# First products of the second layer on GpSimd, their sums two turns later; softplus in pairs

## Chip, cores and metric

The kernel runs on one core of a Trainium2 chip, as one program. The metric is the device time of one execution in microseconds; the median of three runs is given, and a profiled execution beside it.

## What is computed

Two layers, each behind a group norm and with a residual sum, on x of 4 x 256 x 64 x 128 (batch, time, rows, channels) in float32. The first is a pair of selective scans (forward and backward in time) with a gated output, a layer norm and a small MLP; the second makes a kernel per position out of a convolution and mixes with it.

```python
# layer 0, per row: L = 256 steps, 256 inner channels, 16 states
u = silu(causal_conv(xc, cw, cb))
xdbl = u @ Wx.T
dt = softplus(xdbl[..., :8] @ Wdt.T + bdt)
# per step: h = exp(dt * A) * h + (dt * u) * B ; y = sum over n of h * C
y = selective_scan(u, dt, -exp(Al), Bm, Cm, Dv) * silu(z)
...
# layer 1, per position: NH = 8 heads, DK = DV = DD = 16
xp = silu(x @ W1) @ W2                       # q (8 x 16), k (16), v (16), each normed
K_H1 = conv2d(k, H1_w).reshape(-1, DK, DD) + P1
kernel = einsum('xnk,xkd->xnd', q, K_H1)
feature = conv2d(v, H2_w); V_G = conv2d(v, G_w) + I
feature = einsum('xvw,xvd->xwd', V_G, feature)
out = einsum('xnd,xvd->xvn', kernel, feature)
```

## The kernel before

**Layer 0.** The rows are taken two at a time: a group G is 512 columns (two rows of 256 steps), 32 groups make one batch entry, 128 groups the whole. Each group has 32 units (G, i, n), one per direction i and state n, 4096 in all. The main loop (line 993) is one turn per unit k: turn k traces, for the unit three ahead, the broadcast of its C row from DRAM (`rows_of_c`, line 464, on SP's queue) and its operands (`inputs`: four dbt on ScalarE at line 472, a memset of one column on GpSimd at line 476, two exponentials "decay" on ScalarE at line 478); TensorE's transposes of dbt into one of three banks db (`turned`, line 492); the two scans on VectorE (`scanned`, line 504), which read decay from SBUF and db from PSUM; the weighting of the scanned states by C on GpSimd (`weighted`, line 510); and, for the unit two turns back, the transposing sums into the banks y (`added`, line 532). dbt, decay, hs and cc have four buffers each.

**The streams.** All the rest is written as generators that take steps between the units. A `yield 1, n` ends a turn's step, and n is how many of the three free PSUM banks ("mm", lists `free`, `take`, `give`) the next step needs; without them the stream waits. `front` makes a group's operands: transposes and norms, the convolution into u, silu, and per direction dt with its softplus, du = dt times u on GpSimd (line 418) and its transposes. A front starts 50 turns ahead of its group (LEAD); if it is not ready in time, the loop steps all the streams again in the same turn (line 1035). `back` takes the finished y through gate, projection, norms and MLP: xo is written at lines 571 and 574, x1 = MLP + xo at line 615, its statistics and its transposes follow, and x1 goes to DRAM. `project` starts the second layer on chunks of 512 positions: q, k and v, with the squares on GpSimd (line 690) and their sums on VectorE (line 693). A batch entry's chunks can begin when its whole first layer is done. `mix` takes the projected chunks four blocks of 128 positions at a time.

**A block of `mix`.** Filters: TensorE convolves k and v into one bank `fil` (`filters`, line 750). First product: `products` (line 755) multiplies q, repeated over d, with the filter's first 256 columns, repeated over heads, 2048 elements, into the single buffer pr. First sum: line 840 reduces these to ker, 128 columns. Second product (line 755 again) of the filter's other half with ker, and the bank is given back. Second sum at line 851, the outer product at line 766 and the gathering by TensorE at line 777; the result is copied to o at line 862. Between these stand `yield`s, so a block is spread over several turns. While the mixing is behind its plan (line 1023), it has two steps in every fourth turn. Blocks that are left when the loop ends go through `mix_alone`, which has an order of its own and has its first products on GpSimd already (line 925).

**Order.** Instructions go to the engines' queues by a list scheduler, which follows the program's order where operands are ready in its own estimate of time and takes later ones first where they are not. Two things bind it by hand: `tc.keep_in_program_order(ins)` puts an instruction behind the one traced before it on its engine, and `with tc.issue_after(ins)` puts what the block traces on that engine behind `ins`; neither waits for completion. The engines run their queues in order.

**Activation tables.** Exp and Ln share a table; silu, gelu and softplus need others. `both_tables` (line 204) loads the shared one by hand; where a function's table is not there, a load stands on the function's own line. `softplus` (line 305) is called once per group, with the dt of both directions, then takes any waiting gelu.

Of the kernel before, what the change touches and what calls it, by code (L numbers as in the profile page):

```python
# [13 lines left out]
F32 = mybir.dt.float32  # L14
AF = mybir.ActivationFunctionType
ALU = mybir.AluOpType
AX = mybir.AxisListType
# [9 lines left out]
NH, DK, DV, DD = 8, 16, 16, 16  # L27
# [5 lines left out]
COLS = 512  # L33
# [6 lines left out]
def fused_kernel(ctx: ExitStack, tc: tile.TileContext, a: dict, out: bass.AP):  # L40
    nc = tc.nc
# [90 lines left out]
    with tc.tile_pool(name="prep", bufs=1) as prep:  # L132
        w_in = prep.tile([128, DI], F32, name="w_in")
        nc.sync.dma_start(out=w_in, in_=a["W_inT"][:, 0:DI])
        for i, s in enumerate(("", "b")):
# [9 lines left out]
            na = const.tile([128, 2, NS], F32, name=f"neg_a{i}")  # L145
# [16 lines left out]
    p1 = ctx.enter_context(tc.tile_pool(name="p1", bufs=1))  # L162
# [26 lines left out]

    free = list(banks)  # L190
    norms = []

    def take():
        return free.pop(0)
# [4 lines left out]
    def later(turns):  # L199
        for _ in range(turns):  # L200
            yield 1, 0
# [101 lines left out]
            nc.vector.tensor_scalar(to, bank, bias, None, ALU.add)  # L303

    def softplus(*ts):
        for dt in ts:
            nc.scalar.activation(dt, dt, AF.Softplus)  # L307
        gelu()
        both_tables()

# [184 lines left out]
    def scanned(k):  # L495
        G, i, n = units[k]
        st = state[G]
        hs = st["hs", i, n] = p4.tile([128, 2, COLS], F32, name="hs")
        da = st.pop(("da", i, n)).rearrange("d (h s) t -> d h (s t)", h=2)
        for h in range(2):  # L500
            d0, d1, dh = da[:, h, :], dbs[(2 * k + h) % 3], hs[:, h, :]
            if i == 1:
                d0, d1, dh = d0[:, ::-1], d1[:, ::-1], dh[:, ::-1]
            nc.vector.tensor_tensor_scan(dh, d0, d1, 0.0, ALU.mult, ALU.add)  # L504

    def weighted(k):
        G, i, n = units[k]
# [34 lines left out]
    def back(G):  # L542

        b, g = divmod(G, NGRP)
# [25 lines left out]
        xo = p1.tile([128, COLS], F32, name="xo")  # L570
# [40 lines left out]
            )  # L611
        turned_x(m2, xin, add=True)
        yield 1, 0
        x1 = p1.tile([128, COLS], F32, name="x1")
        nc.vector.scalar_tensor_tensor(x1, m2, b2m, xo, ALU.add, ALU.add)
        give(m2)
        yield 1, 1
# [131 lines left out]
                    dst = dst.rearrange("p (k d) -> p d k", k=cn)  # L749
            nc.tensor.matmul(dst, lhsT=lhsT, rhs=wt, start=start and t == 0, stop=t == 2, skip_group_check=True)  # L750

    def products(left, right, na, nb):

        pr = p1.tile([128, na, nb, 16], F32, name="pr")
        nc.vector.tensor_tensor(  # L755
            pr,
            left.rearrange("p (a e) -> p a e", e=16)[:, :, None, :].to_broadcast([128, na, nb, 16]),
            right.rearrange("p (b e) -> p b e", e=16)[:, None, :, :].to_broadcast([128, na, nb, 16]),
            ALU.mult,
        )  # L760
        return pr

    def outer(eng, pr, left, right, na, nb):
# [42 lines left out]
    def mix():  # L806

        blocks = [(K, j) for K in range(B * NCHK) for j in range(CB)]
        fil = None

        def filters(K, j):
            f = take()
            convolved(f[:, 0:256], 0, K, j, True, True)
            convolved(f[:, 256:512], 1, K, j, False)
            return f

        for at, (K, j) in enumerate(blocks):
            if j == 0 and len(cols) > 1:
                return
            w = chunk.get(K)  # L820
            if j == 0 and "operands" not in (w or {}):
                while not ready(K):
                    yield 1, 0
                    if len(cols) > 1:
                        return
                w = chunk[K]
                operands(K)
                yield from later(3)
            if j == 0:
                o = p1.tile([128, CB, C], F32, name="o")  # L830
                x1 = loaded_x1(K)
            qkv = w["qkv"]
            if fil is None:
                yield 1, 1
                fil = filters(K, j)
                yield 1, 0
            pr = products(qkv[:, j, 0 : NH * DK], fil[:, 0:256], NH, DD)
            yield 1, 0
            ker = p1.tile([128, NH * DD], F32, name="ker")
            nc.vector.tensor_reduce(ker.rearrange("p (n d) -> p n d", d=DD), pr, AX.X, ALU.add)  # L840
            yield 1, 0
            pr = products(fil[:, 256:512], ker, DV, NH)
            give(fil)
            fil = None
            yield 1, 1
            gat = take()
            convolved(gat[:, 0:256], 2, K, j, True)
            if j == CB - 1 and len(cols) == 1 and ready(K + 1):
                operands(K + 1)
            nv = p1.tile([128, DV * NH], F32, name="nv")  # L850
            nc.vector.tensor_reduce(nv.rearrange("p (v n) -> p v n", n=NH), pr, AX.X, ALU.add)  # L851
            yield 1, 0
            pr = p1.tile([128, DV, C], F32, name="pr")
            outer(nc.vector, pr, by(gat[:, 0:256]), by(nv, NH), DV, NH)
            give(gat)
            yield 1, 1
            ot = take()
            gathered(ot[:, 0:128], pr, x1[:, j : j + 1, :])
            if j + 1 < CB and free:
                fil = filters(*blocks[at + 1])  # L860
            yield 1, 0
            nc.scalar.copy(o[:, j, :], ot[:, 0:128])
            give(ot)
            if j == CB - 1:
                w["mixed"] = True
                yield 1, 1
                yield from finish(K, o)
# [125 lines left out]
    for k in range(len(units) + LAG):  # L993
        G, at = divmod(k, UNITS)
        b, g = divmod(G, NGRP)
# [118 lines left out]
```

## Time and profile before

| | us |
|---|---|
| median of three runs (19493.19 to 19508.58) | 19500.96 |
| the profiled execution | 19461.56 |
| its span | 19459.8 |
| first scan starts / last scan starts | 198.8 / 18083.6 |
| first sum at line 840, first / last start (376 of them) | 4430.4 / 18189.8 |
| sums of `mix_alone` (line 908), first / last start (136) | 18242.2 / 19447.9 |

| engine, line | what | count | busy us | mean ns |
|---|---|---|---|---|
| GpSimd 510 | weighting | 4096 | 9717.3 | 2375 |
| VectorE 504 | scan | 8192 | 9503.4 | 1203 |
| ScalarE 472 | dbt | 16384 | 7051.8 | 499 |
| ScalarE 478 | decay | 8192 | 5443.3 | 711 |
| TensorE 492 | transposes into db | 32768 | 4999.5 | 284 |
| TensorE 532 | transposing sums into y | 32768 | 4453.2 | 280 |
| GpSimd 418 | du | 256 | 617.6 | 2412 |
| GpSimd 766 | outer products of `mix_alone` | 272 | 544.6 | 2028 |
| ScalarE 204 | table loads by hand | 420 | 538.9 | 1283 |
| ScalarE 307 | table loads at softplus | 195 | 250.2 | 1283 |

How to read it: "busy" is the time in which an engine works on instructions of the program; "idle before" is the engine's idle time just ahead of an instruction, and what is named behind an arrow is the event that ended it ("issue": nothing that the profile shows). Means over the whole run mix stages with different limits, so the same views are also taken over windows, counted in us from the span's start. Some records are missing from a trace: 374 of the 376 first products carry their operands' names.

### The profile page before, as it was taken

What the parts mean: (1) busy time and instruction counts of PE and PEld (TensorE: products, weight loads), DVE (VectorE), ACT (ScalarE), POOL (GpSimd) and SP (SyncE); (2) the same over time, 40 slices, a digit from 0 to 9 for tenths busy, and PEclk for the clock granted to TensorE, in tenths of its full rate; (3) what the DMA queues carried; (4) which work ended last, traced back from release to release, by engine and by line L of the source; (5) the groups of instructions that cost most, each with busy time, mean ns of one, the idle gap of its engine ahead of it and who ended that gap; (6) DMA issues with size and microseconds to landing.
All of it is one profiled execution on the core that took longest, in us unless ns stands there. A gap on an engine that the chain in (4) does not pass through costs nothing. (4 is left out here: it accounts for less than half of the span.)

```text
span 19459.8 us, 310011 instructions
## 1 busy us (share of the span) xinstructions
PE 16942.8 (87%) x109608; PEld 13087.9 (67%) x109608; DVE 16298.0 (84%) x13626; ACT 16155.3 (83%) x31245; POOL 11335.3 (58%) x9001
## 2 busy tenths in 40 slices
PE   6999988888888888888888888888888888888788
PEld 4666666666666666666666666666666666666677
DVE  5877777768898888888888888888888888888788
ACT  6999999998887888888888888888888888888322
POOL 4777666665555555555555555555555555555454
PEclk9999999999999999999999999999999999999899
DMA  2232222222332222222232222322222222232222
GB/s 76 86 87 86 80 79 79 79 81 78 90 87 75 80 85 81 80 83 89 84 82 83 81 78 79 87 80 79 81 84 80 80 86 79 81 86 78 68 72 66
DMA packets 1321091, 1574.85 MB, mean 81 GB/s; under 512 B 343232, under 2 KB 704880, under 8 KB 1319536
## 3 DMA queue, kind: packets, MB, share of 16 engines
q1 hardware_dynamic: 1318000, 1554.40, 27.7%
q8 instruction: 865, 14.17, 0.3%
q14 instruction: 690, 5.65, 0.1%
q10 hardware_dynamic: 1536, 0.63, 0.0%
HBM read 1420.15 MB, written 134.45 MB: 80 GB/s over the span
## 5 line engine op out<-in xcount | busy, mean ns | idle before, releaser
L510 POOL TENSOR_TENSOR hs<-hs,cc 128x1024 f32<-128x1024 f32 x4096 | 9717.3, 2375 | 6891.3 <-issue 3003.3
L504 DVE TENSOR_TENSOR_SCAN hs<-decay,db 128x512 f32<-128x512 f32 x8192 | 9503.4, 1203 | 1262.4 <-PE db L492 844.8
L472 ACT ACTIVATE dbt<-duT,bT 128x256 f32<-128x256 f32 x16384 | 7051.8, 499 | 470.6 <-PE db L492 467.3
L478 ACT ACTIVATE decay<-dt,neg_a 128x510 f32<-128x510 f32 x8192 | 5443.3, 711 | 764.3 <-DVE hs L504 755.1
L492 PE MATMUL db<-ident,dbt 128*128 128x128 f32 x32768 | 4999.5, 284 | 1017.7 <-DVE hs L504 890.8
L492 PEld LDWEIGHTS db<-ident,dbt 128*128 128x128 f32 x32768 | 3860.4, 145 | 2710.4 <-DVE hs L504 1403.8
L532 PE MATMUL y<-ident,hs 128*128 128x128 f32 x32768 | 4453.2, 280 | 2.4 <-POOL hs L510 2.4
L532 PEld LDWEIGHTS y<-ident,hs 128*128 128x128 f32 x32768 | 3868.9, 145 | 156.9 <-issue 140.2
L359 PE MATMUL mm<-hpad,w_cv 128*128 128x512 f32 x4096 | 1937.8, 597 | 37.7 <-ACT hpad L348 14.1
L755 DVE TENSOR_TENSOR pr<-qkv,mm 128x2048 f32<-128x2048 f32 x374 | 852.6, 2280 | 544.0 <-PE mm L750 245.0
L359 PEld LDWEIGHTS mm<-hpad,w_cv 128*128 128x128 f32 x4096 | 702.9, 190 | 592.3 <-issue 521.9
L755 DVE TENSOR_TENSOR pr<-mm,ker 128x2048 f32<-128x2048 f32 x421 | 955.3, 2269 | 4.3 <-ACT ker L932 2.4
L766 DVE TENSOR_TENSOR pr<-mm,nv 128x2048 f32<-128x2048 f32 x374 | 849.3, 2271 | 20.3 <-PE mm L750 17.8
L851 DVE TENSOR_REDUCE nv<-pr 128x128 f32<-128x2048 f32 x376 | 852.3, 2267 | 1.0
L840 DVE TENSOR_REDUCE ker<-pr 128x128 f32<-128x2048 f32 x376 | 851.2, 2264 | 0.3
L777 PE MATMUL mm<-ident,pr 128*128 128x128 f32 x5936 | 751.9, 280 | 82.6 <-DVE pr L766 74.9
L777 PEld LDWEIGHTS mm<-ident,pr 128*128 128x128 f32 x5936 | 683.3, 144 | 208.6 <-DVE pr L766 101.4
L418 POOL TENSOR_TENSOR du<-dt,u 128x1024 f32<-128x1024 f32 x256 | 617.6, 2412 | 301.2 <-ACT dt L307 217.8
L766 POOL TENSOR_TENSOR decay<-qkv,duT 128x1024 f32<-128x1024 f32 x272 | 544.6, 2028 | 385.4 <-ACT duT L920 288.3
L431 PE MATMUL mm<-ident,du 128*128 128x128 f32 x2048 | 383.0, 305 | 334.9 <-POOL decay L476 243.5
L204 ACT ACT_TABLE_LOAD x420 | 538.9, 1283 | 5.6
L519 PEld LDWEIGHTS y<-diag_d,u 128*128 128x128 f32 x4096 | 491.7, 198 | 51.2 <-ACT yt L549 25.3
(284 smaller groups left out, 19239.0 us busy)
## 6 DMA issues: line engine op xcount, KB each, us to landing
cc<-cd SPq DMA_DIRECT2D x4096, 256.0 KB
cols<-kv_img SPq DMA_DIRECT2D x444, 210.0 KB
xin<-in_x SPq DMA_DIRECT2D x256, 256.0 KB
kv_img<-kv_pad SPq DMA_DIRECT2D x896, 64.0 KB
cols<-kv_img SPq DMA_DIRECT2D x222, 252.0 KB
xst<-in_x SPq DMA_DIRECT2D x128, 256.0 KB
x1d<-ot SPq DMA_DIRECT2D x256, 128.0 KB
xt<-x1d SPq DMA_DIRECT2D x128, 256.0 KB
```

Source lines behind the costliest of these rows:

```text
L359: nc.tensor.matmul(cv.rearrange("c (s t) -> c s t", s=SG), lhsT=w_cv[i][:, k, h * 128 : (h + 1) * 128], rhs=hp[:, :, o : o + T], start=k == 0,
L472: nc.scalar.mul(dbt[:, j, :], duT[:, j, :], bT[:, i, j, n : n + 1])
L478: nc.scalar.activation(da[:, h * SG : (h + 1) * SG, lo : lo + T - 1], dt[:, h, :].rearrange("d (s t) -> d s t", s=SG)[:, :, lo : lo + T - ...
L492: last = nc.tensor.transpose(db[:, 128 * j : 128 * (j + 1)], dbt[:, j, 128 * h : 128 * (h + 1)], ident)
L504: nc.vector.tensor_tensor_scan(dh, d0, d1, 0.0, ALU.mult, ALU.add)
L510: nc.gpsimd.tensor_tensor(hs, hs, cc[:, None, :].to_broadcast([128, 2, COLS]), ALU.mult)
L532: nc.tensor.matmul(y[j // 2][:, j % 2, h, :], lhsT=hs[:, h, 128 * j : 128 * (j + 1)], rhs=ident, is_transpose=True, start=False, stop=i == ...
L755: nc.vector.tensor_tensor(pr, left.rearrange("p (a e) -> p a e", e=16)[:, :, None, :].to_broadcast([128, na, nb, 16]), right.rearrange("p ...
L766: eng.tensor_tensor(pr.rearrange("p e (a b) -> p e a b", b=nb), left[:, :, :, None].to_broadcast([128, n, na, nb]), right[:, :, None, :].t ...
L777: nc.tensor.matmul(to, lhsT=p, rhs=ident, is_transpose=True, start=k == 0, stop=stop and k == len(blocks) - 1, skip_group_check=True,)
L840: nc.vector.tensor_reduce(ker.rearrange("p (n d) -> p n d", d=DD), pr, AX.X, ALU.add)
L851: nc.vector.tensor_reduce(nv.rearrange("p (v n) -> p v n", n=NH), pr, AX.X, ALU.add)
```

## The change

The first product goes to GpSimd in two halves, and since that engine does not read the PSUM bank, ScalarE first copies the filter's first 256 columns to a tile ks in SBUF, one turn ahead. The first sum on VectorE is traced two turns after the product instead of one, and is queued behind the scan that was traced last. The second product and all that follows is as before, so the bank `fil` is held for two turns more. x1 is written over xo instead of into a tile of its own. The softplus of the second direction now stands ahead of that of the first, and each is put behind the instruction traced before it on ScalarE.

```diff
+    scans = [None]
...
     def softplus(*ts):
-        for dt in ts:
-            nc.scalar.activation(dt, dt, AF.Softplus)
+
+        for dt in reversed(ts):
+            tc.keep_in_program_order(nc.scalar.activation(dt, dt, AF.Softplus))
         gelu()
         both_tables()
...
-            nc.vector.tensor_tensor_scan(dh, d0, d1, 0.0, ALU.mult, ALU.add)
+            scans[0] = nc.vector.tensor_tensor_scan(dh, d0, d1, 0.0, ALU.mult, ALU.add).ins
...
-        x1 = p1.tile([128, COLS], F32, name="x1")
+        x1 = xo
         nc.vector.scalar_tensor_tensor(x1, m2, b2m, xo, ALU.add, ALU.add)
...
-    def products(left, right, na, nb):
+    def products(left, right, na, nb, eng=None):
 
         pr = p1.tile([128, na, nb, 16], F32, name="pr")
-        nc.vector.tensor_tensor(
-            pr,
-            left.rearrange("p (a e) -> p a e", e=16)[:, :, None, :].to_broadcast([128, na, nb, 16]),
-            right.rearrange("p (b e) -> p b e", e=16)[:, None, :, :].to_broadcast([128, na, nb, 16]),
-            ALU.mult,
-        )
+        for k in range(2 if eng else 1):
+            n = na // 2 if eng else na
+            (eng or nc.vector).tensor_tensor(
+                pr[:, n * k : n * (k + 1)],
+                left.rearrange("p (a e) -> p a e", e=16)[:, n * k : n * (k + 1), None, :].to_broadcast([128, n, nb, 16]),
+                right.rearrange("p (b e) -> p b e", e=16)[:, None, :, :].to_broadcast([128, n, nb, 16]),
+                ALU.mult,
+            )
         return pr
...
-            pr = products(qkv[:, j, 0 : NH * DK], fil[:, 0:256], NH, DD)
-            yield 1, 0
+            ks = p1.tile([128, DD * DK], F32, name="ks")
+            nc.scalar.copy(ks, fil[:, 0:256])
+            yield 1, 0
+            pr = products(qkv[:, j, 0 : NH * DK], ks, NH, DD, nc.gpsimd)
+            yield from later(2)
             ker = p1.tile([128, NH * DD], F32, name="ker")
-            nc.vector.tensor_reduce(ker.rearrange("p (n d) -> p n d", d=DD), pr, AX.X, ALU.add)
+            with tc.issue_after(scans[0]):
+                nc.vector.tensor_reduce(ker.rearrange("p (n d) -> p n d", d=DD), pr, AX.X, ALU.add)
             yield 1, 0
             pr = products(fil[:, 256:512], ker, DV, NH)
```

## Prediction

> **What bounds the kernel now.** I read the page first, then busy time by window, then one steady stretch by line, then DVE's timeline inside it. The page names no engine as the bound:
>
> ```profile
> PE 16942.8 (87%) x109608; PEld 13087.9 (67%) x109608; DVE 16298.0 (84%) x13626; ACT 16155.3 (83%) x31245; POOL 11335.3 (58%) x9001
> ## 2 busy tenths in 40 slices
> ...
> DVE  5877777768898888888888888888888888888788
> ACT  6999999998887888888888888888888888888322
> POOL 4777666665555555555555555555555555555454
> ```
>
> The slices show three stages. In the first eight, ACT is full and the second layer is absent. Then DVE rises, ACT falls a little, and that lasts to slice 37. The last three are the second layer alone, with ACT at 3 and below. The change works in the middle stage, so I cut one window from the first stage and one from the middle (columns: window, length, then busy time and count of PE, PEld, DVE, ACT, POOL, then granted clock):
>
> ```profile
> 1400.00:1974.00 574.00, 530.70 (x3336) 385.61 (x3334) 454.87 (x463) 562.04 (x1091) 406.79 (x330) 0.99 0.29 86
> 11904.20:13371.83 1467.63, 1284.35 (x8342) 997.77 (x8341) 1294.22 (x1031) 1272.44 (x2441) 844.72 (x681) 0.95 0.28 82
> ```
>
> In the first stage ACT is busy for 562.04 of 574, 97.9%, and PE for 92.5%. In the second window DVE, PE and ACT stand at 88.2%, 87.5% and 86.7%, and POOL at 57.6%. That window holds 641 scans; a group has 32 turns of two scans, so it is ten groups of 146.8 us. By line:
>
> ```profile
> L504 DVE TENSOR_TENSOR_SCAN hs<-decay,db 128x512 f32<-128x512 f32 x641 | 741.1, 1202 | 48.8 <-PE db L492 48.4
> L755 DVE TENSOR_TENSOR pr<-qkv,mm 128x2048 f32<-128x2048 f32 x40 | 91.1, 2278 | 59.4 <-issue 49.4 <-PE mm L750 10.0
> L840 DVE TENSOR_REDUCE ker<-pr 128x128 f32<-128x2048 f32 x40 | 90.7, 2267 | 0.0
> L307 ACT ACT_TABLE_LOAD x20 | 25.7, 1283 | 0.4
> L478 ACT ACT_TABLE_LOAD x10 | 12.8, 1283 | 0.2
> ```
>
> Four blocks of the second layer go through each group, and each takes five DVE instructions of 2.27 us; the first, L755 from qkv, is what moves. L307 loads a table twice per group although it has one pair of softplus: an Exp between the two brings a load of its own (L478). DVE's timeline shows how the products sit:
>
> ```profile
> 11957.92 2.32 DVE L504 TENSOR_TENSOR_SCAN hs<-decay,db 128x512 f32<-128x512 f32 x2
> 11960.16 2.27 DVE L766 TENSOR_TENSOR pr<-mm,nv 128x2048 f32<-128x2048 f32 x1
> 11962.34 4.54 DVE L504 TENSOR_TENSOR_SCAN hs<-decay,db 128x512 f32<-128x512 f32 x4
> 11971.83 2.29 DVE L755 TENSOR_TENSOR pr<-qkv,mm 128x2048 f32<-128x2048 f32 x1 [4.94 <-issue]
> 11974.03 1.21 DVE L504 TENSOR_TENSOR_SCAN hs<-decay,db 128x512 f32<-128x512 f32 x1
> ```
>
> A turn with a product is filled by DVE (2.32 + 2.27 us and no gap); the next scan, and with it PE's transposes for the scan after, wait behind it. So the middle stage alternates: DVE ends turns with a product, ACT or PE ends the others.
>
> **The change, part by part.** *First product off DVE.* 376 blocks run in the loop (the page of lines counts L840 376 times), and 376 x 2.278 = 857 us leave DVE, 9.1 per group of 146.8. What that is worth is set by who ends the turns next. If DVE kept its share of 88.2%, a group would take (129.4 - 9.1)/0.882 = 136.4 us. PE has 128.4 us of work per group; at the highest share that the trace shows for it, 92.5%, that is 138.9 us. ACT at 97.9% would need some 129. I take the longest, 138.9: 7.9 us less per group, over 376/4 = 94 groups **743 us less**. The bounds are nothing and 978 (94 x 10.4, DVE's share kept). The 4.94 us gap ahead of the product I count as no gain: PE was working through the convolution and the gathering of the block before, and the transposes for the next scan come behind these.
>
> *Its place on POOL.* Two halves of 1024 elements. The nearest rows are the outer products of the last stage (L766 on POOL, 2.028 us) and the weighting of the scans (L510, 2.375): 4.06 to 4.75 us per block. At 4.75 POOL has 84.5 + 19 = 103.5 us of work in a group of 138.9, 75%. Queued behind the halves are the weightings, du and the squares of qkv. PE waited for weighted scans 2.4 us in all over 32768 transposes (L532), so a weighting late by one half costs nothing; I count zero. If that cover were gone, one half per block in PE's way is 376 x 2.375 = 893 us.
>
> *The copy to ks on ACT.* Between 0.257 us for 128 columns (L862) and 0.417 for 320 (L684): 0.37 each, 1.5 per group. It sits in ACT's queue ahead of the dbt and decay of the next turns and waits for PE's filters as the product did (L755 waited 245.0 for PE and 191.8 for issue in the whole run): 0 to 437 us of ACT idle, 4.6 per group at most, against 19.5 that ACT idles in one now. Zero in the sum; 437 if ACT came to be the bound.
>
> *The sums, two turns later, behind the last scan.* The reduce can no longer stand ahead of that scan, but it still stands in DVE's queue ahead of the following scans, and if POOL is late they wait. The nearest row is the other DVE reduce that takes a POOL result, L693 after the squares: 189.9 us idle in 128, 1.5 each, one turn after its producer. Here two turns lie between, but 4.75 us of POOL work instead of 1.25. The bounds are zero and one late weighting, 2.375. I take 0.5, a third of the row: 376 x 0.5 = **188 us more**.
>
> *Pace.* A block goes through two turns more, and its filters hold one of three PSUM banks that much longer. Four blocks per 32 turns with a double step in each fourth turn are 10 steps a block, 6 of them its own, so some 4 are waits now, which can swallow the two added. None swallowed is 12 steps, and 376 x 2/12 = 63 blocks would move to the last stage, where a block takes (19447.9 - 18242.2)/135 = 8.9 us. I take 0.6 steps, 21 blocks: 188 us at the end, and 21 x 9.1 x 743/857 = 165 less in the loop, **some 25 more**. Bounds: zero, and 562 with no relief.
>
> *Softplus in pairs.* One load of L307 and the one of L478 go, 2.57 us of ACT per group. ACT is not what ends the group in my sum, so nothing; were it the bound, 94 x 2.57 = 242 less. That dt0 is ready later delays its du by a few us, in a front that starts 50 turns ahead of its group.
>
> *x1 written over xo.* No instruction more or less; xo stays in use until the next transposes, and the next group's xo comes a group later. Zero.
>
> **A rule against it.** The row: L574, the only frequent DVE instruction in the loop that reads two SBUF tiles, takes 1735 ns where its sibling L571, with one operand in PSUM, takes 730, so 128 x 1.0 us is lost already. The Trainium skill, "SBUF — State Buffer", section "Who interferes with whom", says that such an instruction and a GpSimd instruction that reads SBUF lock each other out for the whole instruction. By the row, a POOL busier by a third adds some 40 us. By the rule, it is at most one product half each time, 128 x 2.375 = 304. I leave both outside the sum: there is one such instruction per group, and in the sum PE ends the group. The skill's "GPSIMD Engine Reference", section "4.1 Engine selection", tells not to put elementwise work there, about twice as slow; the rows say the same of the duration, but time on an idle engine is not time on the path.
>
> **Sum.** 743 less, 188 and 25 more: 530 less. The profiled execution took 19461.56 (span 19459.8), so 18,931; the median of the runs shown lies 39 above it: **18,970**.
>
> **Rivals.** *The reduce becomes the stall (slower).* Place: L840 behind scan k+2 with the halves still on POOL, a weighting between them. For it: L693 already shows DVE placed too early behind POOL, and where no product stands between, two turns take 4.54 us (four scans in a row above), less than 4.75 + 2.375 of POOL work. Against: the mean turn is 146.8/32 = 4.6. It decides from (743 - 25)/376 = 1.9 us per reduce; at 2.5 it gives 940 - 718 = 222 more, 19,720. *PE or ACT ends the turns anyway.* For: both stand within 2 points of DVE, and DVE's idle pockets end on PE. Against: in the first stage both run fuller. At a PE share of 89% a group is 144.3, 235 less, and with the 188 and 25 the time is near 19,480; I give this 19,330 to 19,540. *All of it arrives.* DVE's share kept and no stall: 978 less, 18,520. That the pin does not bring the pair together (it only forbids going earlier, an Exp may still come between) costs at most the 242 that I did not count.
>
> **How the numbers follow.** Forecast, 18,700 to 19,330: 0.56. All of it arrives: 0.10. PE or ACT: 0.18, of which 0.10 is faster by over 0.2%, 0.07 within and 0.01 slower. The reduce stalls: 0.16. A measurement of this kernel tells about 0.2%, 39 us, from no change. Faster 0.76, same 0.07, slower 0.17. The range reaches from near the second bound of the gain, 18,560, to 19,560, a little into the slower case.
>
> **What would show it.** Right: in a steady window L755 from qkv is gone from DVE, a POOL row writes pr at 2.0 to 2.4 us per half, the group is near 139 to 141 us with PE above 90%, L307 loads once per group, L840 waits for POOL about 0.5 us each. Wrong: L840 idle of 2 us or more each; PE waiting for hs at L532; group length unchanged with idle before L504 grown; fewer than 340 reduces at L840 and a last stage longer than 1.6 ms.

## The result: 0.42% slower

| | us | runs |
|---|---|---|
| before, on the same chip | 19497.07 (19480.84 to 19508.58) | 6 |
| after | 19568.33 (19564.4 to 19576.39) | 6 |
| ratio | 1.0042, interval 1.0032 to 1.0052 | |

The change costs 71 us, 1.8 times the 39 us that the prediction took as the smallest difference that can be told. 18,970 was predicted, so the forecast was wrong by 598 us and on the wrong side; what happened is the rival in which the sum becomes the stall.

The page of after (its span is 19566.6 us; the granted clock 0.950, before 0.956). The profile calls TensorE PE, VectorE DVE, ScalarE ACT and GpSimd POOL. In the new line numbers the scan is L506, the products L759, the first sum L848, the copy to ks L842, the weighting L512:

```profile
PE 16873.5 (86%) x109676; PEld 13165.8 (67%) x109676; DVE 15475.3 (79%) x13250; ACT 16036.9 (82%) x31479; POOL 13044.2 (67%) x9753
DVE  5887777767777888888877887887787887887788
POOL 4777666666666777766766666666676666666454
```

DVE lost 822.7 us of work against before (16298.0 to 15475.3) and fell from 84% to 79%; its middle stage went from eights to a mixture of sevens and eights. POOL took the work over and rose from 58% to 67%. Only POOL is nearer to full than before, and it is far from it, and yet the run is longer. So it is idle time that grew, and the question is at which instruction. The same two windows as in the prediction (window, length, busy time and count of PE, PEld, DVE, ACT, POOL, clock):

```profile
1400.00:1974.00 574.00, 528.02 (x3366) 389.78 (x3364) 458.43 (x469) 566.76 (x1102) 411.72 (x333) 0.99 0.30 87
11904.20:13371.83 1467.63, 1260.15 (x8179) 991.37 (x8178) 1180.23 (x967) 1222.10 (x2402) 1000.59 (x743) 0.95 0.29 80
```

The first stage, with no second layer in it, is nearly as it was. In the second window DVE is at 80.4%, PE at 85.9%, ACT at 83.3%: all three lower than before (88.2, 87.5, 86.7). The window holds 625 scans where it held 641: a group takes 1467.63 x 64 / 625 = 150.3 us, against 146.8 before and 138.9 in the prediction. The same window by line (busy, mean ns, then idle time just before the instruction and what ended it):

```profile
L506 DVE TENSOR_TENSOR_SCAN hs<-decay,db 128x512 f32<-128x512 f32 x625 | 724.5, 1203 | 128.5 <-PE db L494 78.6 <-ACT dbt L474 9.6 <-ACT dt L300 9.2
L770 DVE TENSOR_TENSOR pr<-mm,nv 128x2048 f32<-128x2048 f32 x40 | 91.3, 2282 | 53.6 <-PE mm L752 42.8 <-issue 9.1 <-ACT dbt L474 1.7
L848 DVE TENSOR_REDUCE ker<-pr 128x128 f32<-128x2048 f32 x39 | 89.0, 2283 | 73.0 <-POOL pr L759 51.9 <-POOL decay L478 20.5
```

The sum's 0.0 us of idle became 73.0 in 39 sums, 1.9 each (the memset at L478 that the row names is an instruction of POOL as well). Over the whole run:

```profile
L506 DVE TENSOR_TENSOR_SCAN hs<-decay,db 128x512 f32<-128x512 f32 x8192 | 9499.5, 1204 | 1854.2 <-PE db L494 1302.0 <-ACT decay L480 115.9 <-ACT dbt L474 104.9
L848 DVE TENSOR_REDUCE ker<-pr 128x128 f32<-128x2048 f32 x372 | 848.5, 2281 | 769.8 <-POOL pr L759 593.8 <-POOL decay L478 174.2
L759 POOL TENSOR_TENSOR pr<-qkv,ks 128x1024 f32<-128x1024 f32 x744 | 1751.8, 2375 | 215.4 <-ACT ks L842 133.0
L770 DVE TENSOR_TENSOR pr<-mm,nv 128x2048 f32<-128x2048 f32 x368 | 838.0, 2277 | 190.3 <-PE mm L752 132.6 <-issue 25.9 <-ACT decay L480 17.6
```

The same rows of before, over the whole run:

```profile
L504 DVE TENSOR_TENSOR_SCAN hs<-decay,db 128x512 f32<-128x512 f32 x8192 | 9503.4, 1203 | 1262.4 <-PE db L492 844.8 <-ACT decay L478 105.2 <-ACT dbt L472 99.7
L755 DVE TENSOR_TENSOR pr<-qkv,mm 128x2048 f32<-128x2048 f32 x374 | 852.6, 2280 | 544.0 <-PE mm L750 245.0 <-issue 191.8 <-ACT o L862 39.6
L840 DVE TENSOR_REDUCE ker<-pr 128x128 f32<-128x2048 f32 x376 | 851.2, 2264 | 0.3
L766 DVE TENSOR_TENSOR pr<-mm,nv 128x2048 f32<-128x2048 f32 x374 | 849.3, 2271 | 20.3 <-PE mm L750 17.8 <-issue 2.3
```

DVE's books, from these rows of after and of before: the first products are gone with 853 us of work and 544 us of idle ahead of them, 1397 together. New idle time is 592 ahead of the scans (1262.4 to 1854.2), 770 ahead of the first sums (0.3 to 769.8) and 170 ahead of the outer products (20.3 to 190.3), 1532 together. So DVE gave back all that it was relieved of. But these books alone do not say which of the three costs time: idle ahead of a scan can also mean only that DVE no longer ends the turns (e3 below has as much of it). The timeline shows one of the stalls, first on DVE (start, length, instruction, idle before it):

```profile
10677.96 5.66 DVE L506 TENSOR_TENSOR_SCAN hs<-decay,db 128x512 f32<-128x512 f32 x5
10687.44 2.29 DVE L848 TENSOR_REDUCE ker<-pr 128x128 f32<-128x2048 f32 x1 [3.83 <-POOL pr L759]
10689.65 1.21 DVE L506 TENSOR_TENSOR_SCAN hs<-decay,db 128x512 f32<-128x512 f32 x1
```

and then POOL in the same microseconds:

```profile
10680.41 2.37 POOL L512 TENSOR_TENSOR hs<-hs,cc 128x1024 f32<-128x1024 f32 x1 [3.05 <-issue]
10682.74 4.67 POOL L759 TENSOR_TENSOR pr<-qkv,ks 128x1024 f32<-128x1024 f32 x2
10687.35 2.38 POOL L512 TENSOR_TENSOR hs<-hs,cc 128x1024 f32<-128x1024 f32 x1
```

The filter's copy was ready at 10678.06, but POOL stood idle for 3.05 us with a weighting at the head of its queue; that weighting began when the second of DVE's five scans had ended (10677.96 + 2 x 1.13 = 10680.2; the profile names no releaser, so this is read from the times). Behind it came the two halves, 4.67 us. DVE meanwhile had three more scans, some 3.4 us, and then the sum at the head of its queue, which waited until the halves were done. From the end of the second scan POOL needed 2.37 + 4.67 us and DVE had 3.4: the difference, 3.6, is nearly all of the 3.83 us in brackets. The next scan was behind the sum. The sum was traced two steps after the product, and the tie put it behind the last scan; neither says that POOL is done. This stall is one of the long ones: the mean is 2.07 us, and a table at the end of the experiments sorts all of them.

### The profile page after: what moved, and what is told of

Its sections match the earlier page's. It is cut to its first block, busy times and chain, and to the rows that moved or that the text cites. A ratio compares the mean times of both kernels' runs of the same rounds, so it can differ in the third digit from the quotient of the medians.

```text
span 19566.6 us, 309719 instructions
## 1 busy us (share of the span) xinstructions
PE 16873.5 (86%) x109676; PEld 13165.8 (67%) x109676; DVE 15475.3 (79%) x13250; ACT 16036.9 (82%) x31479; POOL 13044.2 (67%) x9753
## 5 line engine op out<-in xcount | busy, mean ns | idle before, releaser
L512 POOL TENSOR_TENSOR hs<-hs,cc 128x1024 f32<-128x1024 f32 x4096 | 9706.0, 2371 | 5236.4 <-issue 2083.7
L506 DVE TENSOR_TENSOR_SCAN hs<-decay,db 128x512 f32<-128x512 f32 x8192 | 9499.5, 1204 | 1854.2 <-PE db L494 1302.0
L494 PE MATMUL db<-ident,dbt 128*128 128x128 f32 x32768 | 4899.7, 283 | 1324.0 <-DVE hs L506 1242.8
L480 ACT ACTIVATE decay<-dt,neg_a 128x510 f32<-128x510 f32 x8192 | 5454.1, 712 | 651.0 <-DVE hs L506 641.7
L759 POOL TENSOR_TENSOR pr<-qkv,ks 128x1024 f32<-128x1024 f32 x744 | 1751.8, 2375 | 215.4 <-ACT ks L842 133.0
L848 DVE TENSOR_REDUCE ker<-pr 128x128 f32<-128x2048 f32 x372 | 848.5, 2281 | 769.8 <-POOL pr L759 593.8
L770 DVE TENSOR_TENSOR pr<-mm,nv 128x2048 f32<-128x2048 f32 x368 | 838.0, 2277 | 190.3 <-PE mm L752 132.6
L759 DVE TENSOR_TENSOR pr<-mm,ker 128x2048 f32<-128x2048 f32 x407 | 924.9, 2273 | 6.1
```

The lines of the kernel that those rows point to most:

```text
L480: nc.scalar.activation(da[:, h * SG : (h + 1) * SG, lo : lo + T - 1], dt[:, h, :].rearrange("d (s t) -> d s t", s=SG)[:, :, lo : lo + T - ...
L494: last = nc.tensor.transpose(db[:, 128 * j : 128 * (j + 1)], dbt[:, j, 128 * h : 128 * (h + 1)], ident)
L506: scans[0] = nc.vector.tensor_tensor_scan(dh, d0, d1, 0.0, ALU.mult, ALU.add).ins
L512: nc.gpsimd.tensor_tensor(hs, hs, cc[:, None, :].to_broadcast([128, 2, COLS]), ALU.mult)
L759: (eng or nc.vector).tensor_tensor(pr[:, n * k : n * (k + 1)], left.rearrange("p (a e) -> p a e", e=16)[:, n * k : n * (k + 1), None, :].t ...
L770: eng.tensor_tensor(pr.rearrange("p e (a b) -> p e a b", b=nb), left[:, :, :, None].to_broadcast([128, n, na, nb]), right[:, :, None, :].t ...
```

## Experiments

Each run stands beside runs of the kernel before on its own chip, and "minus before" and the ratio are taken there; the medians of different rows can come from different chips. "Idle at the sum" and "idle at the scans" are DVE's, of the whole run; "blocks" are those that go through the loop.

| run | median us | minus before | ratio, interval | idle at the sum | idle at the scans | blocks |
|---|---|---|---|---|---|---|
| before | | 0 | 1 | 0.3 | 1262.4 | 376 |
| after | 19568.33 | +71 | 1.0042, 1.0032 to 1.0052 | 769.8 | 1854.2 | 372 |
| e1 softplus alone | 19285.63 | -194 | 0.9901, 0.9887 to 0.9915 | 0.2 | 1176.3 | 376 |
| e2 before, no first product | 18860.78 | -619 | 0.9682, 0.9669 to 0.9695 | 587.9 | 1307.5 | 376 |
| e3 after, no first product | 18699.02 | -781 | 0.9601, 0.9588 to 0.9614 | 9.7 | 1860.6 | 372 |
| e4 sum three turns later | 19464.27 | -15 | 0.9992, 0.9984 to 1.0001 | 528.1 | 2147.0 | 340 |
| e5 products run unread | 18769.14 | -699 | 0.9641, 0.9628 to 0.9654 | 9.5 | 1859.9 | 372 |
| e6 no tie | 20096.32 | +629 | 1.0324, 1.0310 to 1.0338 | 1317.6 | 1757.4 | 372 |
| e7 half on each engine | 19081.54 | -386 | 0.9800, 0.9787 to 0.9813 | 169.0 | 1520.2 | 372 |
| e8 four turns, more steps | 19389.85 | -78 | 0.9959, 0.9946 to 0.9973 | 386.5 | 2120.8 | 364 |
| e9 three turns, same pace | 19182.02 | -299 | 0.9847, 0.9833 to 0.9860 | 363.8 | 1927.0 | 372 |
| e10 half on each, three turns | 18944.16 | -537 | 0.9722, 0.9709 to 0.9735 | 55.2 | 1581.0 | 372 |
| e11 the change without pairing | 19585.48 | +104 | 1.0055, 1.0042 to 1.0067 | 771.5 | 1841.3 | 372 |

The theory after the result: the relief of DVE is real, and the sum's wait for POOL gives it back. The rivals: there was no relief (PE or ACT ends the turns anyway); POOL's added work delays the weightings; the copy, the two turns or x1 over xo cost it; the softplus in pairs costs something.

**e1. The pairing alone.** The kernel before with the changed softplus and nothing else.

```diff
-        for dt in ts:
-            nc.scalar.activation(dt, dt, AF.Softplus)
+        for dt in reversed(ts):
+            tc.keep_in_program_order(nc.scalar.activation(dt, dt, AF.Softplus))
```

> The kernel before with nothing but the two softplus reversed and pinned. Both theories: one table load at the softplus line per group instead of 195 in all, none at the decay line. My sum counted it at nothing (19,500); if ScalarE ended the turns, up to 242 us less (19,255). It says how much of the changed kernel's time is owed to the pairing.

194 us faster. The line of e1 that loads the table of softplus:

```profile
L307 ACT ACT_TABLE_LOAD x128 | 164.2, 1283 | 1.8
```

195 loads became 128, one per group, and the 51 at L478, 17 at L695 and 11 at L696 are gone: 146 loads of 1.283 us, 187 us of ACT. The lines of before that went:

```profile
L478 ACT ACT_TABLE_LOAD x51 | 65.4, 1283 | 0.9
L695 ACT ACT_TABLE_LOAD x17 | 21.8, 1283 | 0.3
L696 ACT ACT_TABLE_LOAD x11 | 14.1, 1283 | 0.2
```

The time fell by as much, so ACT, at 86.7% in the steady window, did end part of the turns; the prediction had set this part at nothing.

**e2. What the first product costs in the order of before.** The product is left out, so ker is not computed from q: the sum reads the filter in its bank, repeated over heads, with the same 2048 elements.

```diff
-            pr = products(qkv[:, j, 0 : NH * DK], fil[:, 0:256], NH, DD)
+            pr = fil[:, 0:256].rearrange("p (d e) -> p d e", e=16)[:, None, :, :].to_broadcast([128, NH, DD, 16])
```

> The kernel before with the multiplication by q left out: the first sum reads the filter straight from the bank, 2048 elements as before, and no turn is moved. It is what the first product off VectorE is worth if nothing takes its place. Theory POOL-wait (VectorE's relief is real and was given back at the sum, which waits for POOL): 600 to 750 us less than before, 18,750 to 18,900. Theory PE (TensorE ends the turns whatever VectorE does): at most 150 less, 19,350 to 19,500, with idle before the scans grown by about what was taken away.

619 us less: DVE was worth relieving, so the rival in which PE or ACT ends the turns anyway is out. Not all of the 619 need be the product's: with the softplus as before, e2 has 162 loads at L307, 18 at L478, 15 at L695 and 11 at L696, 68 fewer than before, 87 us of ACT. If these are worth what such loads were worth in e1, the product alone brought about 530. The first sum of e2 inherits the product's wait for the filters:

```profile
L840 DVE TENSOR_REDUCE ker<-mm 128x128 f32<-128x2048 f32 x374 | 854.3, 2284 | 587.9 <-PE mm L750 578.5 <-PE db L492 6.9
```

The product had 544 us of idle ahead of it; the sum has 588 now. So the prediction was right to count this gap as no gain.

**e3. The same in after.** The halves on POOL are left out (ker is not computed from q), the sum reads ks; copy, two turns, tie, x1 and pairing stay.

```diff
-            pr = products(qkv[:, j, 0 : NH * DK], ks, NH, DD, nc.gpsimd)
+            pr = ks.rearrange("p (d e) -> p d e", e=16)[:, None, :, :].to_broadcast([128, NH, DD, 16])
```

> The changed kernel with the two halves on GpSimd left out: the sum reads the copy ks itself, so that it waits for nothing on POOL; copy, turns, tie and pairing as in the change. Theory POOL-wait: the 770 us of idle before the sum vanish, 18,800 to 18,950, near the run without the product in the old order. Theory PE: 19,450 to 19,570, the idle going to the scans. If it stays well above the run in the old order, the two turns and the longer held bank are the loss.

781 us below before, the fastest of all, and 162 below e2, which ran beside it. Of what stands between the two, the pairing takes away 78 loads at the four lines named at e2, 100 us of ACT, so about as much time by the rate of e1. That would leave some 60 us that the copy, the two turns, the tie and x1 over xo gained together; by this estimate they did not cost time. One reason can be seen: the sum of e2 waits 588 us for the filters, the sum of e3 9.7 for the copy. None of these parts was tried alone. What makes the difference to after is in POOL's halves or in the wait for them. The sum's line of e3:

```profile
L848 DVE TENSOR_REDUCE ker<-ks 128x128 f32<-128x2048 f32 x372 | 841.0, 2261 | 9.7 <-ACT ks L842 9.7
```

The scans' idle is 1860.6 here and 1854.2 in after: this entry of the books above is no loss. It is there in the fastest kernel as well.

**e4. One turn more for the sum.**

```diff
-            yield from later(2)
+            yield from later(3)
```

> The changed kernel with the sum three turns after the product instead of two. Theory POOL-wait: idle before the sum falls from 770 us to below 250 and the time to 19,150 to 19,350, less some 10 to 20 blocks moved to the last stage. Theory PE: idle moves to the scans, 19,550 to 19,650. Theory pace and banks: slower, above 19,650.

Some 86 us better than after by the distances to before (104 by the medians), and not to be told from before. The first sum of e4 in the loop, and the sum of the blocks left for the end:

```profile
L848 DVE TENSOR_REDUCE ker<-pr 128x128 f32<-128x2048 f32 x340 | 772.7, 2273 | 528.1 <-POOL pr L759 437.2 <-POOL decay L478 90.5
L916 DVE TENSOR_REDUCE nv<-pr 128x128 f32<-128x2048 f32 x172 | 392.1, 2280 | 2.0
```

The wait is 1.55 us per sum, from 2.07, and 32 blocks moved to the end (172 sums at L916, 140 in after): the last stage takes 1635 us, 203 more. A step added to a block without care for the pace is paid at the end. The two effects are mixed here; e9 keeps the number of steps.

**e5. POOL's work without the wait.** The products run on POOL, in pieces of 768, 768 and 512 elements, into a tile that nobody reads; the sum reads ks, so ker is not computed from q. For the room, h3 and ot share a buffer.

```diff
-            pr = products(qkv[:, j, 0 : NH * DK], ks, NH, DD, nc.gpsimd)
+            prx = p1.tile([128, 3, 16, 16], F32, name="prx")
...
+            nc.gpsimd.tensor_tensor(prx[:, 0:n], ..., ALU.mult)
+            pr = ks.rearrange("p (d e) -> p d e", e=16)[:, None, :, :].to_broadcast([128, NH, DD, 16])
```

> As the run of the change without its first product, but GpSimd does the multiplication all the same, into a tile that nobody reads (three pieces of 768, 768 and 512 elements, since a whole 4 KB do not fit; two tiles of the back stream share a buffer to make room). POOL is as full as in the change, and the sum waits for nothing on it. Theory POOL-wait: near the run without the product, 18,700 to 18,850. Rival, POOL's load itself (weightings, du and squares late, so that TensorE and VectorE wait for these): 19,200 or more, up to the 19,568 of the change.

699 us below before, 82 less of a gain than e3 (70 by the medians alone). The lines of e5:

```profile
L506 DVE TENSOR_TENSOR_SCAN hs<-decay,db 128x512 f32<-128x512 f32 x8192 | 9496.7, 1203 | 1859.9 <-PE db L494 1262.6 <-PE y L534 124.5 <-ACT decay L480 116.1
L846 POOL TENSOR_TENSOR prx<-qkv,ks 128x768 f32<-128x768 f32 x744 | 1362.1, 1831 | 191.8 <-ACT ks L842 170.3 <-DVE hs L506 1.4
L856 DVE TENSOR_REDUCE ker<-ks 128x128 f32<-128x2048 f32 x372 | 840.6, 2260 | 9.5 <-ACT ks L842 9.5
```

POOL does 1362.1 + 474.7 (372 pieces of 512) = 1836.8 us of products, more than the 1751.8 of after, and this costs some 70 to 82 us. What is between e5 and after, 1.0042 - 0.9641 = 0.0401 or some 780 us, is the sum's dependence on the products: 760 us of idle ahead of it. In 323 of the 372 blocks the sum stands as many scans down DVE's queue as in after, and in 48 of the others earlier, so it is not its place that spared it the wait. This is the run that decides. The weightings that stand behind the halves are not the cost; the instruction on DVE that waits for them is.

**e6. Without the tie.** The sum is traced two turns later as in after, but the scheduler may put it where it likes.

```diff
-            with tc.issue_after(scans[0]):
-                nc.vector.tensor_reduce(...)
+            nc.vector.tensor_reduce(...)
```

> The changed kernel without the tie of the sum to the last scan. If the tie is what puts the sum too early or late, the time moves: faster than 19,450 if it holds the sum in front of ready scans, slower than 19,650 if it protects. My theory: the sum stands where the scheduler believes POOL to be done, which is behind that scan anyway, so 19,500 to 19,640 and idle before the sum of 700 to 850 us.

A miss: 629 us slower than before, 558 worse than with the tie. The sum of e6:

```profile
L848 DVE TENSOR_REDUCE ker<-pr 128x128 f32<-128x2048 f32 x372 | 850.2, 2285 | 1317.6 <-POOL pr L759 985.7 <-POOL decay L478 330.3
```

3.54 us per sum. DVE's instruction order, counted in the trace as scans ahead of each sum, shows why: in 171 of the 372 blocks the sum stands where it stood with the tie, in 174 it stands two scans earlier, in 23 one or four earlier, in 4 one later. Left to itself, the scheduler puts the sum ahead of scans that could have run. The tie protects, but it reaches too short. Why the scheduler puts it there (its own time for POOL's products, or what it thinks that DVE could do in between) was not tried.

**e7. Half as much to wait for.** The first half of the product goes to POOL, the second stays on DVE and reads the bank.

```diff
-            pr = products(qkv[:, j, 0 : NH * DK], ks, NH, DD, nc.gpsimd)
+            for h, (eng, right) in enumerate(((nc.gpsimd, ks), (nc.vector, fil[:, 0:256]))):
+                eng.tensor_tensor(pr[:, 4 * h : 4 * (h + 1)], ..., ALU.mult)
```

> The changed kernel with only the first half of the product on GpSimd and the second on VectorE, straight from the bank. POOL is done 2.3 us earlier. Theory POOL-wait: idle before the sum falls from 2.07 us each to some 0.5 (190 us), VectorE takes back 429 us of work, worth about 310 at the rate of the run without the product: 19,150 to 19,300. If the load or the ScalarE copy were the loss: 19,450 or more.

386 us below before, though DVE has half of the work back (372 x 1.2 us). The sum of e7:

```profile
L855 DVE TENSOR_REDUCE ker<-pr 128x128 f32<-128x2048 f32 x372 | 843.1, 2266 | 169.0 <-POOL pr L846 100.0 <-POOL decay L478 68.4
```

0.45 us per sum in place of 2.07.

**e8. Four turns, and more steps to make up for them.**

```diff
-            yield from later(2)
+            yield from later(4)
...
-        for _ in range(2 if behind and at % 4 == 1 else 1):
+        for _ in range(2 if behind and at % 2 == 1 else 1):
```

> The changed kernel with the sum four turns after the product and, while the mixing is behind, two steps in every second turn instead of every fourth, so that the pace holds. Theory POOL-wait: idle before the sum below 150 us, 372 blocks or more in the loop, 18,750 to 19,000, the fastest that computes everything. If the longer held bank costs: 19,200 or more, with idle moved to the scans and the fronts late.

A miss: 78 us below before, where far more was expected. The sum and the scans of e8:

```profile
L848 DVE TENSOR_REDUCE ker<-pr 128x128 f32<-128x2048 f32 x364 | 826.3, 2270 | 386.5 <-POOL pr L759 307.2 <-POOL decay L478 78.7
L506 DVE TENSOR_TENSOR_SCAN hs<-decay,db 128x512 f32<-128x512 f32 x8192 | 9498.5, 1203 | 2120.8 <-PE db L494 1467.6 <-ACT decay L480 121.8 <-issue 119.6
```

The sum still waits 1.06 us each, and the scans have 261 us more of idle ahead of them than in e5, most of it for PE. Doubling the steps in every second turn changes where all of the mixing stands, not only the sum; that the extra steps crowd PE's work into fewer turns is a reading of this line and was not tried by itself. The expectation also took steps for turns. With two steps in every second turn, four steps are two or three turns, and the trace has no sum with the eight scans of four turns between (the table below).

**e9. One turn later, the pace kept.** The turn that the sum takes more is taken from between it and the second product.

```diff
-            yield from later(2)
+            yield from later(3)
...
-            yield 1, 0
             pr = products(fil[:, 256:512], ker, DV, NH)
```

> The changed kernel with the sum three turns after the product, and the second product in the same turn as the sum, so that a block takes as many turns as in the change. The run with three turns and one turn more per block had 1.55 us of idle at each of 340 sums and moved 32 blocks to the last stage, some 200 us. Theory POOL-wait: idle before the sum 450 to 600 us instead of 770, 372 blocks in the loop, 19,250 to 19,400. Rival, that the turn saved brings the chain sum, product, sum close together and its own waits come back: 19,500 or more.

299 us below before, better than expected, with 372 blocks in the loop as in after. The sum of e9:

```profile
L848 DVE TENSOR_REDUCE ker<-pr 128x128 f32<-128x2048 f32 x372 | 844.6, 2270 | 363.8 <-POOL pr L759 311.7 <-POOL decay L478 51.9
```

One step more took 406 us of idle away, and the time went down by 370 against after by the distances to before (386 by the medians). At e4 the same step took away 242, and the last stage gave 203 back.

**e10. Both.** The edits of e7 and e9 together.

> The kernel with half of the product on each engine (19,082), with the same shift: sum three turns after, second product in the turn of the sum. It had 169 us of idle at the sum. Theory POOL-wait: at most these 169 us can go, so 18,920 to 19,080. Rival as in the run beside it: 19,100 or more.

18944.16 us (18931.67 to 18954.03): 2.8% faster than before, with all of the computation in it, and faster than any other run that computes everything. The sum of e10 and the half that is on DVE:

```profile
L855 DVE TENSOR_REDUCE ker<-pr 128x128 f32<-128x2048 f32 x372 | 841.9, 2263 | 55.2 <-POOL pr L846 39.7 <-POOL decay L478 15.4
L846 DVE TENSOR_TENSOR pr<-qkv,mm 128x1024 f32<-128x1024 f32 x367 | 441.0, 1202 | 152.6 <-ACT ks L842 135.6 <-PE mm L781 4.4 <-PE db L781 3.8
```

The wait is 0.15 us per sum, and 441 us of product are back on DVE: about half of the relief is given up, and hardly any of the rest is lost at the sum.

**e11. The change without the pairing.** The softplus of before in the kernel after.

> The change without the pairing of the softplus: the other part alone. The pairing alone was worth 194 us on the kernel before. If the two parts add, 19,568 + 194 = 19,762, some 1.4% slower than before, and idle before the sum near 770 us. If the pairing is worth less where VectorE waits for POOL anyway, 19,570 to 19,680.

17 us above after by the medians, 33 by their distances to before; the two intervals overlap, so the pairing's worth inside the change is not clear of noise. The loads at softplus in e11:

```profile
L309 ACT ACT_TABLE_LOAD x152 | 195.0, 1283 | 2.7
```

152 loads where after has 128 and before had 195; with 19 at L480 and 5 elsewhere, pairing saves 48 loads here, 62 us of ACT, where it saved 146 and 187 us in e1. Inside the change the softplus stand closer by themselves, so there is less to save. And 17 to 33 us for 62 of ACT is also a lower rate than that of e1; that the sum's wait hides it is a reading that was not tried.

**Put together.** Four runs have the same blocks in the loop and all of the product's work on POOL, and differ in how long the sum waits for POOL. From e5 to e9, after and e6, idle at the sum is 10, 364, 770 and 1318 us, and the time against before is -699, -299, +71 and +629. The steps are 354, 406 and 548 of idle, and 400, 370 and 558 of time: in these four runs each microsecond that DVE waits at the sum goes with a microsecond of the run, within 13%. The granted clock falls along the same row (0.966, 0.952, 0.950, 0.934), so a part of the first and the last step may be the clock's; between e9 and after it was nearly the same, and there 406 us of idle are 370 of time.

How long a sum waits can be read from its place. The weighting ahead of the first half of a product needs two scans; the table counts, in the order of the traces, how many scans DVE has between the second of these and the sum (two scans are one turn), with the number of blocks and the mean idle time at the sum:

| run | three scans or fewer | four | five or six |
|---|---|---|---|
| after | 126, 3.78 us | 229, 1.24 us | 17, 0.49 us |
| e4 | 107, 3.76 us | 73, 1.58 us | 160, 0.07 us |
| e6 | 289, 4.01 us | 79, 1.97 us | 4, 0.83 us |
| e8 | 63, 3.66 us | 105, 1.25 us | 196, 0.13 us |
| e9 | 32, 4.02 us | 126, 1.72 us | 214, 0.09 us |

The wait goes by the place, much alike in every run: six scans are nearly enough, four are not, and three or fewer cost nearly 4 us. The runs differ in how many blocks they have in each column. So "two turns later" in the program was less than two turns in DVE's queue for 126 of the 372 blocks of after, and these make 476 of its 770 us. A second step in the same turn brings the sum a turn nearer, and the scheduler can put the product behind a later weighting; which of the two did it was not taken apart.

## The prediction, step by step

**Relief of DVE, 743 less: near in size, somewhat too much.** e2 measured 619 in the old order (0.8 of the 743, and 0.7 without what its fewer table loads are worth), and the way from before to e5, which has all parts but the sum's wait, is 699, with pairing in it. The prediction's 743 with its 25 for the pace is 718.

**The floor that PE sets, 138.9 us: nearly right in size, by a share that PE does not reach.** It came from the share of the first stage, 92.5%. (That stage ends with slice nine rather than eight: the first sum starts at 4430 us, the slices are 486.5 long.) Most of the middle stage as one window shows how full the engines get, first in before:

```profile
4400.00:17000.00 12600.00, 10992.28 (x71017) 8487.31 (x71017) 10981.09 (x8819) 10784.77 (x20704) 7157.11 (x5774) 0.96 0.29 82
```

then in e2:

```profile
4400.00:17000.00 12600.00, 11254.58 (x74227) 8756.34 (x74228) 10711.15 (x8865) 11130.61 (x21577) 7490.99 (x6040) 0.97 0.29 86
```

in e3:

```profile
4400.00:17000.00 12600.00, 11267.45 (x74933) 8784.20 (x74932) 10760.23 (x8946) 11267.65 (x22103) 7550.76 (x6109) 0.98 0.29 87
```

and in after:

```profile
4400.00:17000.00 12600.00, 10868.46 (x70641) 8501.98 (x70640) 10178.97 (x8440) 10633.82 (x20834) 8655.57 (x6428) 0.95 0.29 82
```

This stretch has 5686 scans in e2, 12600 x 64 / 5686 = 141.8 us per group; in e3 5752 and 140.2, in after 5427 and 148.6, in before 5436 and 148.3. So leaving out the product brings 6.5 us per group where 7.9 were expected, and with the rest of the change it is 8.1. PE stands at 89.3% in e2 and 89.4% in e3, ACT at 88.3 and 89.4%: no engine gets past 90% in this window, and PE did not end the turns alone, or ACT's relief by the pairing would have brought nothing (e1). At a share of 89% the rival had 144.3 us per group. The groups were shorter because PE's own work per group fell as well, from 129.4 us in before to 126.7 in e2 and 125.4 in e3, with the clock going from 0.96 to 0.97 and 0.98. So the size came out by two errors that offset each other: a share that PE does not reach, and work that was taken as fixed.

**Placement on POOL, nothing: nearly right.** Half by half it took 2.375 us, the upper of the two rows. e5 against e3 puts the cost at 70 to 82 us, not the 893 of a cover gone. PE's transposing sums show the cover, in after:

```profile
L534 PE MATMUL y<-ident,hs 128*128 128x128 f32 x32768 | 4467.2, 280 | 9.6 <-POOL hs L512 5.4 <-POOL decay L478 4.2
```

9.6 us of PE waiting for weighted scans, where it was 2.4. (In the same row of e9, which has DVE waiting less, it is 112.3: the cover gets thinner, and is not gone.) The Trainium skill's advice in "GPSIMD Engine Reference", section "4.1 Engine selection", against elementwise work on that engine fits the outcome of this change, but not by its ground: the longer duration (4.75 us against 2.28, about twice, as the page has it) was mostly hidden as long as nobody waited for it (e5), and the wait was the cost (after).

**The copy to ks, nothing; x1 over xo, nothing; the pace, 25.** The copy in after:

```profile
L842 ACT COPY ks<-mm 128x256 f32<-128x256 f32 x367 | 134.0, 365 | 85.8 <-PE mm L752 66.1 <-POOL pr L759 6.1 <-issue 5.7
```

It took 0.365 us, with 85.8 us of ACT idle ahead of it, of the 437 that were the bound. e3 against e2 leaves no cost for these together with the two turns, rather a gain of some 60 us by the estimate at e3; none of them was tried alone. Four blocks moved to the last stage, not 21.

**The sum's wait, 188: this is the step that failed.** "I take 0.5, a third of the row: 376 x 0.5 = 188 us more." It is 769.8 / 372 = 2.07 us each, 582 us more than the term had, and this is all but 16 of the 598 by which the forecast is off. (The 16 are small because the other errors nearly cancel: the pairing gave more than nothing, and the relief and POOL's load cost against the sum.) The bounds, 0 to 2.375, held it; the choice between them was wrong, and in its direction too. The row that it went by (the sums of the squares, 1.5 us each) has 1.25 us of POOL's work ahead of it, the sum has 4.67, and the two turns were taken as time for POOL, as if they were two turns of DVE's queue. In 126 blocks they were not, and these make 476 of the 770 us. In the 229 where they were, the sum still waits 1.24 us. The reason is that POOL's queue moves with DVE's scans: the halves stand behind a weighting that needs scans just done, so POOL starts late, and then, in the stall shown, needs 2.37 + 4.67 us while DVE has 3.4 left. What counts is the work on both queues from the last event that they share, not the turns between two lines of the program.

**The softplus in pairs, nothing: wrong alone, right inside the change.** One load per group came, as the pairing promised. On the kernel before it gave 194 us, near the 242 that had been named for a bound ACT; in the change it gave 17 to 33, which is not clear of noise.

**The rivals.** "The reduce becomes the stall" named the place, the weighting and the point from which it decides, 1.9 us per sum. Its own arithmetic at 2.07 gives 770 - 718 = 52 more; 71 came. One detail differs: in the stall shown, the weighting stands ahead of the two halves, not between them; between them it stands in 39 of the 372 blocks. Of the signs of being wrong, the 2 us at L848 came. Idle before the scans grew as well, at an unchanged length of the group, but that sign misleads: it is as large in e3, the fastest run. "PE or ACT ends the turns anyway" fell with e2 and e3. "All of it arrives" fell too: even e3, with no product at all and the pairing, gains 781, not 978. "The pin does not pair" fell by the 128 loads.

**The SBUF rule, left outside the sum: rightly.** The row it was weighed by is in after:

```profile
L576 DVE SCALAR_TENSOR_TENSOR xo<-xo,L_conv_b,xg 128x512 f32<-128x512 f32 x128 | 175.1, 1368 | 1.9
```

It is shorter than before (1735 ns), though POOL has 1709 us more work; in e1 and e2 it took 1597 and 1606 with POOL's work as before, so it moves without POOL, too. The price that was worked out from "SBUF — State Buffer", section "Who interferes with whom", up to 304 us, did not appear; what else lies beside this instruction changed as well, so the rule itself is not tested by it.

## What to carry to other kernels

Moving work from a busy engine to an idle one has two prices: what the work costs on the idle engine, and what the instruction that reads it back costs on the busy one if it stands in an in-order queue ahead of work that could have run. Here the first was some 75 us and the second 770, and only the second turned a gain into a loss: before such a move, add up what stands in the giving engine's queue ahead of the reader against the taker's queue, from the last event that both wait for. Where they do not match, moving half and putting the reader further back, without lengthening the round (e10), gained 537 us where the whole move lost 71, with the softplus in pairs in both. And count the distance in the reader's queue and not in the program: here two steps of a stream could be one turn.

## Not expected of the hardware

The mean granted clock of TensorE was not the same for the same matrix work (109676 matmul records in each of these runs): 0.973 in e3, 0.966 in e5, 0.963 in e10, 0.950 in after, 0.934 in e6, and PE's busy time follows it (16568.0 us in e3, 16873.5 in after, 17091.0 in e6). It falls together with the speed of these kernels, but does not alone set it: e9 ran at 0.952 and after at 0.950, and they are 386 us apart, while before had 0.956. Whether longer waits lower the clock, or what else does, stays open.

The DVE instruction with two SBUF operands took 1735 ns before, 1368 in after, 1334 in e5 and 1321 in e10, all of which have a busier POOL than before, and 1606 in e2, which has not.
